# A BF16 ramp of places made once for both layers, and new step orders for layer 1, in a two-layer attention kernel

## The chip, the cores and the metric

The kernel runs on one core of a Trainium2 chip. The core has five engines that run side by side and meet through semaphores: TensorE (PE) for matrix products and transposes, VectorE (DVE) and ScalarE (ACT) for elementwise work, GpSimd (POOL) for elementwise work and indirect transfers, and SyncE (SP), which here only issues transfers. ACT and POOL issue transfers too. The metric is the device time of one execution in microseconds.

## What is computed

Two layers in sequence on x of shape (8, 512, 32, 32), so 8 batches of 512 channels and 1024 tokens. All data is float32. In the reference, cut to what matters:

```python
# layer 0: group norm, 8-head attention over all 1024 tokens, projection, residual
h = group_norm(x, 32 groups) * gn_w + gn_b
q, k, v = split(qkv_w @ h + qkv_b)
x = x + proj_w @ (softmax(q.T k / 8) v) + proj_b

# layer 1: attention among the 256 tokens of greatest norm
q, k, v = wq @ x, wk @ x, wv @ x
importance = sum(x * x over channels)
idx = top_k(importance, 256)
q_sel, k_sel, v_sel = q[idx], k[idx], v[idx]
q_sel, k_sel = layer_norm(q_sel), layer_norm(k_sel)
attended = softmax(clip(q_sel k_sel.T / sqrt(512))) v_sel
v[idx] = attended
out = x + wo @ v
```

## The kernel before, in words

Layer 0 runs as 64 units (4 head pairs x 2 halves of the queries x 8 batches). An order written out by hand, `SLOT`, lists the steps of one unit with an offset of units for each step; each engine gets its instructions in that order. A ring of 14 score buffers (`scored`, tag `e`) holds the exponentials: `sc` takes one, the sum on POOL (L1339) and the product with the values on PE (L1350) give it back. `constants()` is called at the start of unit 2: two small vectors, a triangular mask, and the token numbers (two iotas on POOL, then a copy on DVE, L226). The last units mix in the first steps of layer 1 for batch 0. The last residual additions of layer 0 are at L1121 (tile `xr_last`), its last scaling on POOL at L1402.

Layer 1 runs batch by batch in software pipelining. `BATCH` is the order of one period: a word such as `back4---` is step `back` number 4 of the batch three before, `row4+` that of the batch after. `END` is the order of the last stretch, where batches 4 to 7 are finished (there `row3-` belongs to batch 6, `row1` to batch 7). Both are walked in program order, and every engine takes its own instructions in that order and waits where an input or a buffer is not ready. The steps, with their lines in the profile:

- Rows: `row` transposes 128 tokens (PE, L273), `square` takes their norms (ACT, L277) and `keep` copies them (ACT, L283) into one of four `xT` buffers, `put` stores them to DRAM (issued by ACT, L287, `sx<-xT`). `finite` cleans the norms (DVE), `spread` lays them out as a row (PE, L301), `imp` copies it (ACT, L307).
- Places: `count` (DVE, L320 to L330) counts for each token how many come before it; `place` (DVE, L436) adds the counts; `pick` (DVE, L451) compares a ramp 0..255 with each place, four instructions of 128x256 per step, into BF16 one-hot tiles. The ramp was a float32 tile `iota_f` in a pool of layer 1, written by an iota on POOL (L444) when the first `pick` is reached. `holder` (PE, L459) multiplies the one-hot tiles with the token numbers, `who` (DVE, L467) turns them into indices, `getx` (POOL, L475) gathers the selected rows.
- Values, by seven products of halves: `xs` (POOL, L395) forms sums of token blocks, 8 operations per step, in two alternating halves of a buffer; `va` to `vf` are the products (PE, L405); `ka`, `kb`, `kc`, `ke` copy them (ACT, L419); `kd`, `kf`, `kg` add (DVE, L423); `vput` stores them (issued by ACT, L431), `getv` gathers the selected ones (POOL, L475).
- Attention: `selt`, `selk` (PE L503, ACT L509), `qk` (PE, L519), `stats`, `root`, `norm` (DVE L526 to L529, ACT L534, DVE L541 to L548), `normt`, `scale` (PE L559, ACT L570), `score` (PE, L581), `clip` (DVE, L590 to L594), `exp` (ACT, L602), `probt`, `probk` (PE L614, ACT L619), `att`, `attk` (PE L628, ACT L635), `attput` (SP, L641).
- Output: `fetch` gathers attended rows into the values (POOL, L647), `back` transposes (PE, L663), `add` adds the residual and stores (DVE L671, SP L673).

All PE results of layer 1 go through a ring of eight PSUM banks, handed out in program order: a step that takes a bank waits for the step that emptied it last. `load_x1` (SP, L236) loads the tokens of a batch into buffers that alternate between two sets, at the start of each period.

Of the kernel before, what the change touches and what calls it, by code (L numbers as in the profile page):

```python
# [20 lines left out]
P = 128  # L21
# [44 lines left out]
back6--- row3 square1 xs1 back4--- keep2 square3 back7--- va1 inv-- put2 va0 keep3 put4 row0  # L66
keep1 add6--- ka1 add7--- ka0 put1 put3 att0-- xs0 vb1 vb0 kb0 vc0 row6 square0 kb1 add4---
square6 holder- vd0 who- add3--- kc0 keep6 row7 keep0 row5 square5 kg0 vd1 att1-- keep5 square7
getx- keep7 ve0 finite kf1 kc1 attk1-- kf0 va2 attk0-- xs2 attput-- fetch7-- kd0 fetch4--
spread0 imp0 vc1 fetch3-- ka2 spread1 va3 selt0- imp1 selk0- count1 fetch6-- count7 selt1-  # L70
selk1- fetch2-- vb2 kg1 vf1 fetch5-- vput1- count4 kf2 qk1- ke1 count0 ve1 qk0- qk2- xs3 ka3
put0 stats1- vb3 kd1 root1- back5-- norm1- stats0- kb2 put7 vput2- vput4- fetch1-- count3 vput5-
add5-- stats2- root0- qk3- norm0- vd2 vput7- vput0- stats3- root2- kc2 fetch0-- back1-- kb3
root3- vf0 normt0- vput6- ke0 norm2- vd3 back2-- back0-- normt1- vput3- put5 add1-- scale0-
scale1- vc2 vf2 norm3- normt2- count6 ke2 getv- vc3 normt3- add2-- kc3 kg2 add0-- scale2- kg3
scale3- score0- count2 score1- put6 row4+ square4+ ve3 clip- row1+ row2+ keep4+ ve2 exp0- kd3
vf3 kd2 kf3 probt- count5 place back3-- pick1 square2+ pick0 ke3 probk-
"""
END = """
square1- inv--- row7- keep2- back6---- put4- row6- put2- keep1- square7- xs3- row3- row0-  # L80
att1--- put1- keep7- put7- square3- holder-- add3---- row5- attk1--- va3- keep3- square5- row0
keep5- square0- who-- square6- put5- back7---- back4---- vput2-- add7---- finite- add6----
att0--- keep6- spread0- spread1- getx-- add4---- ka3- imp0- row7 keep0- row1 selt0-- imp1- row4
selk0-- square7 selt1-- kf3- put3- put0- selk1-- keep7 count4- count3- vput7-- square4 square1
put7 keep4 xs2- qk0-- count0- attk0--- stats0-- qk1-- count6- va2- stats1-- keep1 attput---
put6- fetch5--- count5- ka2- root1-- kf2- square0 norm1-- keep0 vput4-- qk2-- vb3- vb2- put1
fetch1--- stats2-- put0 row2 kb2- row6 count2- put4 root2-- square2 vd2- square6 row3 kb3- qk3--
fetch7--- square3 keep2 fetch2--- norm2-- fetch6--- count1- kc2- vf2- root0-- vc2- norm0-- row5
vput6-- ke2- square5 kg2- keep3 normt0-- vd3- keep5 kc3- stats3-- root3-- vput1-- vc3- count7-
va0- ve2- scale0-- fetch0--- vput5-- fetch4--- finite norm3-- normt1-- fetch3--- spread1 kd2-  # L90
ka0- put5 imp1 normt3-- normt2-- xs0- scale3-- spread0 kg3- place- pick1- vf3- scale1-- va1-
keep6 pick0- imp0 back7--- holder- scale2-- score1-- score0-- count5 vb0- back6--- who- ve3-
count3 clip-- kb0- vd0- back0--- ka1- getx- back3--- ke3- vput3-- add6--- kf0- vput0-- xs1- vb1-
add7--- back2--- add3--- kc0- put6 selt0- vf0- vc0- exp0-- add2--- kd3- count6 inv-- selt1-
# [52 lines left out]
def attention_then_topk_attention(  # L147
# [293 lines left out]
    def pick(b, j):  # L441
        if "iota" not in w:
            w["iota"] = pools["up"].tile([P, TOP], F32, tag="iota", name="iota_f")
            nc.gpsimd.iota(  # L444
                w["iota"], pattern=[[1, TOP]], base=0, channel_multiplier=0,
                allow_small_or_imprecise_dtypes=True,
            )
# [1182 lines left out]
```

## Time and profile before

| | |
|---|---|
| median of 4 runs | 2372.77 us (2372.18 to 2372.96) |
| profiled execution | 2370.7 us, span from first to last instruction 2369.0 us |
| busy share of the span | PE 98%, DVE 80%, ACT 62%, POOL 60% |
| mean granted TensorE clock | 0.997 of full |
| layer 1 begins on PE | 1918.28 us from the span's start |
| one steady period of layer 1 | 56.7 us, PE busy 56.54 us of it |

Times in profile lines are microseconds from the span's start, unless a column says ns. In a line of groups or of the timeline stand engine, source line, operation, output and inputs; a square bracket holds the engine's idle time before it and what ended that idle time. In a line of waits stand the waiter, whom it waited for, total us, times, and the longest. The lines themselves are shown in the prediction.

### The profile page before, as it was taken

How to read it: one execution, taken by the hardware profiler on the slowest of the kernel's cores; microseconds unless marked ns; L12 is line 12 of the kernel's file. 1: busy time of each engine (PE TensorE's matmuls, PEld its weight loads, DVE VectorE, ACT ScalarE, POOL GpSimd, SP SyncE). 2: the span in 40 equal slices, each digit the busy share in tenths (PEclk: the TensorE clock that was granted, in tenths of full speed). 3: DMA queues.
4: the chain of work that ended last, by engine and by line, in shares of the span. 5: the costliest groups of instructions: out<-in, count | busy, mean ns of one | idle time of the engine just before them, and what ended most of it. 6: DMA issues, size and time to landing. Idle time of an engine off the chain costs nothing.

```text
span 2369.0 us, 36766 instructions
## 1 busy us (share of the span) xinstructions
PE 2324.0 (98%) x13164; PEld 1053.6 (44%) x13164; DVE 1883.4 (80%) x3019; ACT 1477.9 (62%) x2024; POOL 1432.6 (60%) x890
## 2 busy tenths in 40 slices
PE   7999999999999999999999999999999999999998
PEld 3333443344334333433443344334433357777766
DVE  4889888988888788888988898888777366777774
ACT  3678766776777577657776776677666534444622
POOL 2668655866676677657765776676656634444334
PEclk9999999999999999999999999999999999999999
DMA  5112222322221222222222222221323443666655
GB/s 196 48 44 69 71 77 72 102 63 73 82 91 53 84 79 88 57 79 79 90 68 77 88 79 61 84 68 57 102 79 117 150 158 120 218 223 226 215 170 172
DMA packets 201238, 244.43 MB, mean 103 GB/s; under 512 B 41930, under 2 KB 111306, under 8 KB 201056
## 3 DMA queue, kind: packets, MB, share of 16 engines
q1 hardware_dynamic: 175392, 198.51, 26.4%
q10 hardware_dynamic: 18144, 31.48, 3.6%
q0 software_dynamic: 7520, 12.09, 1.9%
q8 instruction: 105, 1.72, 0.3%
q14 instruction: 77, 0.63, 0.1%
HBM read 181.42 MB, written 73.14 MB: 107 GB/s over the span
## 4 chain that ended last, share of the span: by engine, by line
PE 87%; DVE 6%; ACT 2%; DMA 2%; POOL 1%; issue 1%; another core or an unknown queue 0%; SPq 0%; ACTq 0%; DVEq 0%; POOLq 0%
PE sc L1272 18%; PE av L1350 16%; PE g L1031 14%; PE g L898 10%; PE g L1071 7%; PE b_px L405 5%; PE b_pp L519 4%; DVE high L1286 2%; PE b_py L405 2%; PE den L1366 1%; DVE e L1331 1%; PE b_sc L581 1%; PE b_pa L628 1%; PE first L898 1%; PE b_po L663 1%
## 5 line engine op out<-in xcount | busy, mean ns | idle before, releaser
L1339 POOL TENSOR_TENSOR es<-es,e 128x1024 f32<-128x1024 f32 x384 | 910.9, 2372 | 162.3 <-ACT e L1334 145.4
L1331 DVE TENSOR_TENSOR e<-e,ns 128x1024 f32<-128x1024 f32 x512 | 608.6, 1204 | 6.7 <-ACT ns L1327 6.6
L1280 ACT COPY e<-sc 128x1024 f32<-128x1024 f32 x512 | 501.1, 1016 | 167.1 <-DVE high L1286 98.9
L1334 ACT ACTIVATE e<-e 128x1024 f32<-128x1024 f32 x512 | 533.1, 1062 | 100.2 <-DVE e L1331 93.7
L1286 DVE TENSOR_TENSOR high<-sc,high 128x1024 f32<-128x1024 f32 x384 | 469.0, 1221 | 114.2 <-PE sc L1272 88.9
L1272 PE MATMUL sc<-q,k 64*128 64x512 f32 x2048 | 515.1, 618 | 11.1 <-DVE high L1286 8.6
L1350 PE MATMUL av<-e,v 128*64 128x512 f32 x2048 | 490.2, 597 | 1.1 <-ACT e L1334 0.5
L1339 POOL TENSOR_TENSOR es<-e,e 128x1024 f32<-128x1024 f32 x64 | 152.5, 2383 | 447.4 <-ACT e L1334 447.4
L1272 PEld LDWEIGHTS sc<-q,k 64*128 64x128 f32 x2048 | 173.3, 185 | 285.0 <-issue 151.4
L1350 PEld LDWEIGHTS av<-e,v 128*64 128x64 f32 x2048 | 136.1, 136 | 288.0 <-issue 236.9
L1031 PE MATMUL g<-wqkv,mix_qk 128*64 128x512 f32 x960 | 230.9, 602 | 1.3 <-POOL wqkv L943 1.3
L898 PE MATMUL g<-o,wp 128*64 128x512 f32 x912 | 206.8, 595 | 0.0
L1031 PE MATMUL g<-x,mix_qk 128*64 128x512 f32 x720 | 169.8, 592 | 0.0
L1031 PEld LDWEIGHTS g<-wqkv,mix_qk 128*64 128x64 f32 x960 | 60.9, 136 | 155.3 <-issue 114.2
L898 PEld LDWEIGHTS g<-o,wp 128*64 128x64 f32 x912 | 63.0, 137 | 135.4 <-issue 132.9
L519 PE MATMUL b_pp<-w,selT 128*128 128x512 f32 x256 | 114.2, 593 | 0.0
L1121 DVE SCALAR_TENSOR_TENSOR xr<-g,pb,xr 128x512 f32<-128x512 f32 x56 | 42.1, 751 | 81.5 <-PE g L898 80.7
L1286 DVE TENSOR_TENSOR high<-sc,e 128x1024 f32<-128x1024 f32 x64 | 77.3, 1208 | 34.2 <-ACT e L1280 34.1
L1402 POOL TENSOR_TENSOR o<-o,ri 128x512 f32<-128x512 f32 x64 | 81.7, 1277 | 31.2 <-DMA ri<-rid 29.1
L419 ACT COPY V<-b_px 128x256 f32<-128x256 f32 x112 | 39.8, 374 | 95.7 <-PE b_px L405 89.4
L647 POOL DMA_INDIRECT V<-sa,at x64 | 64.5, 1007 | 56.1 <-DMA sa<-att 27.7
L1031 PEld LDWEIGHTS g<-x,mix_qk 128*64 128x64 f32 x720 | 51.6, 137 | 102.9 <-issue 89.9
(227 smaller groups left out, 2868.9 us busy)
## 6 DMA issues: line engine op xcount, KB each, us to landing
nb<-negd SPq DMA_DIRECT2D x128, 256.0 KB
x<-in_x_dram SPq DMA_DIRECT2D x32, 512.0 KB
ri<-rid SPq DMA_DIRECT2D x128, 128.0 KB
sx<-xT ACTq DMA_DIRECT2D x64, 256.0 KB
mix_qk<-mixd SPq DMA_DIRECT2D x120, 128.0 KB
xr<-in_x_dram SPq DMA_DIRECT2D x58, 256.0 KB
x1d<-xr SPq DMA_DIRECT2D x58, 256.0 KB
sv<-V ACTq DMA_DIRECT2D x56, 256.0 KB
```

Source lines behind the costliest of these rows:

```text
L405: nc.tensor.matmul(out_, left, w["products"][n][:, k], start=(first and k == 0), stop=(k == 1), skip_group_check=True,)
L519: nc.tensor.matmul(pp, tiles["selT", b][:, k, ts(rb, P)], w["qk"[which]][:, k, :], start=(k == 0), stop=(k == CT - 1),)
L898: nc.tensor.matmul(out[r, :], wide_[:, r], moving, start=(k == 0), stop=(k == CT - 1),)
L1031: nc.tensor.matmul(pt[r, :], weights[:, k, r], moving[:, k, :], start=(first and k == 0), stop=(k == 1), skip_group_check=True,)
L1071: nc.tensor.matmul(pt[ts(r, HD), ts(j, P)], tokens[:, k, j * P + r * HD : j * P + r * HD + HD], weights[:, k, :], start=(first and j + k = ...
L1272: nc.tensor.matmul(sc[:, hh, :], ks[p][r, ts(j, P)], qs[p][r, ts(hf, HALF)], start=True, stop=True,)
L1280: nc.scalar.copy(raw[t, j], banks["s", t, j])
L1286: nc.vector.tensor_tensor(high[t], banks["s", t, j], raw[t, 0] if j == 1 else high[t], ALU.max)
L1331: nc.vector.tensor_tensor(raw[t, j], raw[t, j], high[t], ALU.add)
L1334: nc.scalar.activation(raw[t, j], raw[t, j], AF.Exp, scale=QK_SCALE)
L1339: nc.gpsimd.tensor_add(sums[t], raw[t, 0] if j == 1 else sums[t], raw[t, j])
L1350: nc.tensor.matmul(avs[t][HD * hh : HD * hh + HD, :], vs[p // 2][:, j, (p % 2) * P + HD * hh : (p % 2) * P + HD * hh + HD], e[:, hh, :], s ...
```

## The change

The ramp moves into `constants()`: an iota writes it as float32 into a score buffer that is free at that moment, a copy turns it into a BF16 constant tile `places`, and `pick` compares that tile with the places. The iota at the first `pick` and its tile are gone. The scratch tile `four` in layer 0 has one buffer in place of two, which is as large (512 bytes per partition) as `places`. `BATCH` and `END` hold the same steps as before in another order.

```diff
 BATCH = """
-back6--- row3 square1 xs1 back4--- keep2 square3 back7--- va1 inv-- put2 va0 keep3 put4 row0
-keep1 add6--- ka1 add7--- ka0 put1 put3 att0-- xs0 vb1 vb0 kb0 vc0 row6 square0 kb1 add4---
-square6 holder- vd0 who- add3--- kc0 keep6 row7 keep0 row5 square5 kg0 vd1 att1-- keep5 square7
-getx- keep7 ve0 finite kf1 kc1 attk1-- kf0 va2 attk0-- xs2 attput-- fetch7-- kd0 fetch4--
-spread0 imp0 vc1 fetch3-- ka2 spread1 va3 selt0- imp1 selk0- count1 fetch6-- count7 selt1-
-selk1- fetch2-- vb2 kg1 vf1 fetch5-- vput1- count4 kf2 qk1- ke1 count0 ve1 qk0- qk2- xs3 ka3
-put0 stats1- vb3 kd1 root1- back5-- norm1- stats0- kb2 put7 vput2- vput4- fetch1-- count3 vput5-
-add5-- stats2- root0- qk3- norm0- vd2 vput7- vput0- stats3- root2- kc2 fetch0-- back1-- kb3
-root3- vf0 normt0- vput6- ke0 norm2- vd3 back2-- back0-- normt1- vput3- put5 add1-- scale0-
-scale1- vc2 vf2 norm3- normt2- count6 ke2 getv- vc3 normt3- add2-- kc3 kg2 add0-- scale2- kg3
-scale3- score0- count2 score1- put6 row4+ square4+ ve3 clip- row1+ row2+ keep4+ ve2 exp0- kd3
-vf3 kd2 kf3 probt- count5 place back3-- pick1 square2+ pick0 ke3 probk-
+inv-- keep2 vput6- square1 back7--- row3 vput3- back6--- keep1 row6 put2 xs1 square3 va1 put1
+keep3 xs0 att0-- put4 back4--- put3 add3--- ka1 va0 vb1 add4--- ka0 vb0 vc0 kb0 add6--- attk0--
+row5 row7 kb1 holder- kf0 vd0 square6 who- square5 add7--- kf1 kc0 square7 vd1 kg0 row0 square0
+keep0 finite keep6 ve0 getx- att1-- vf0 kc1 spread0 keep5 attk1-- attput-- xs2 vput1- imp0
+spread1 fetch5-- fetch2-- kd0 imp1 vf1 va2 ka2 va3 vc1 count1 ke1 vput0- count0 vb2 kg1 fetch6--
+selt0- selk0- fetch7-- ve1 fetch4-- keep7 fetch0-- selt1- selk1- vput4- count4 vput5- count7
+qk1- kb2 ka3 stats1- qk0- xs3 ke0 put6 back5-- count3 qk2- vput7- qk3- root1- stats0- norm1- vb3
+vc2 put7 root0- stats2- vput2- norm0- kf2 fetch1-- root2- add5-- back1-- stats3- root3- norm2-
+vd2 kc2 add1-- kb3 normt0- normt1- vf2 fetch3-- scale0- put5 back2-- vd3 scale1- norm3- normt2-
+getv- ke2 normt3- back0-- scale2- vc3 kc3 scale3- score1- score0- count2 add0-- put0 add2--
+row4+ kg3 kg2 ve3 square4+ count6 clip- keep4+ row2+ vf3 kd3 ve2 kf3 exp0- row1+ probt- ke3 kd1
+kd2 count5 square2+ place pick1 back3-- probk- pick0
 """
 END = """
-square1- inv--- row7- keep2- back6---- put4- row6- put2- keep1- square7- xs3- row3- row0-
-att1--- put1- keep7- put7- square3- holder-- add3---- row5- attk1--- va3- keep3- square5- row0
-keep5- square0- who-- square6- put5- back7---- back4---- vput2-- add7---- finite- add6----
-att0--- keep6- spread0- spread1- getx-- add4---- ka3- imp0- row7 keep0- row1 selt0-- imp1- row4
-selk0-- square7 selt1-- kf3- put3- put0- selk1-- keep7 count4- count3- vput7-- square4 square1
-put7 keep4 xs2- qk0-- count0- attk0--- stats0-- qk1-- count6- va2- stats1-- keep1 attput---
...
-vb1 add5-- add2-- attput kb1 kf1 vc0 vd0 fetch2 back4- vd1 add7-- kc0 kc1 kf0 vf0 kg0 vc1 add4-
-fetch6 kd3 ve0 back6- fetch3 kg1 ve1 kd0 ke0 back3- back1- add6- fetch4 fetch0 kd1 fetch1 vf1
-vf3 ke1 fetch5 back5- back2- back7- back0- back4 add3- back6 add1- add2- add5- back2 add0- back0
-ke3 fetch7 add7- add4 add6 back5 add2 back1 back7 add0 back3 add5 add7 add3 add1
+keep2- xs3- square1- row3- row7- row6- inv--- put4- att1--- square7- back7---- put2- keep7-
+keep1- row0- put7- holder-- put1- add3---- who-- attk1--- square3- row5- square6- back4----
+getx-- keep3- back6---- att0--- square5- keep5- va3- keep6- add4---- square0- keep0- finite-
+put0- add7---- add6---- put5- row1 put3- spread0- imp0- spread1- row0 imp1- row7 selt0-- square1
+selt1-- selk0-- attk0--- ka3- vput2-- selk1-- attput--- vput4-- count3- va2- keep1 square7 keep7
+xs2- count5- put7 qk0-- square0 count0- fetch6--- qk1-- count6- vput3-- row4 vput7-- stats0--
...
+fetch6- vb1 kb0 add4- vd0 kb1 kf0 vd1 fetch4- kc0 kf1 kc1 add7-- add3-- vf0 vc0 kg0 vc1 ve0 kg1
+kd0 back6- add6- fetch3 fetch6 fetch2 ke0 ve1 fetch4 kd1 back1- add1- vf1 ke1 fetch0 vf3 fetch1
+back2- back5- back7- back0- back3- add5- back4 ke3 add7- add2- add3- back6 fetch5 fetch7 back0
+back2 add0- add4 add6 add0 back7 back3 back5 add7 back1 add5 add1 add3 add2
 """
@@ -209,7 +209,14 @@
     before = const.tile([P, P], F32, tag="before", name="before")
     token = const.tile([P, NB, 2], BF16, tag="token", name="token")
 
-    def constants():
+    places = const.tile([P, TOP], BF16, tag="places", name="places")
+
+    def constants(spare):
+        nc.gpsimd.iota(
+            spare, pattern=[[1, TOP]], base=0, channel_multiplier=0,
+            allow_small_or_imprecise_dtypes=True,
+        )
+        nc.vector.tensor_copy(places, spare)
         w["ln_w"] = vector_of(ln_w, CT, "lw")
         w["ln_b"] = vector_of(ln_b, CT, "lb")
         make_lower_triangular(nc, before, val=1.0, diag=False)
@@ -439,17 +446,11 @@
 
 
     def pick(b, j):
-        if "iota" not in w:
-            w["iota"] = pools["up"].tile([P, TOP], F32, tag="iota", name="iota_f")
-            nc.gpsimd.iota(
-                w["iota"], pattern=[[1, TOP]], base=0, channel_multiplier=0,
-                allow_small_or_imprecise_dtypes=True,
-            )
         for i in range(NB // 2):
             nb = j * (NB // 2) + i
             t = get("rp", ("pick", b, nb), [P, TOP], "pick", NB, BF16)
             nc.vector.tensor_scalar(
-                t, w["iota"], tiles["place", b][:, nb : nb + 1], None, ALU.is_equal
+                t, places, tiles["place", b][:, nb : nb + 1], None, ALU.is_equal
             )
 
     def holder(b, _):
@@ -1305,7 +1306,9 @@
 
 
                 r = high.pop(t)
-                four = sp.tile([BLOCKS, P // BLOCK, BLOCK], F32, tag="four", name=f"four_{t}")
+                four = sp.tile(
+                    [BLOCKS, P // BLOCK, BLOCK], F32, tag="four", name=f"four_{t}", bufs=1
+                )
                 for a in range(P // BLOCK):
                     nc.vector.transpose(four[:, a, :], r[ts(a, BLOCK), :])
                 neg = sp.tile([BLOCKS, BLOCK], F32, tag="neg", name=f"neg_{t}")
@@ -1556,7 +1559,8 @@
                         load_x(1)
                         combine_weights()
                     if t == 2:
-                        constants()
+                        constants(spare("places")[:, :TOP])
+                        scored.give("places")
                     if t == UNITS - 3:
                         load_layer1()
                     for name, ahead, j in order:

```

## The prediction

> **What bounds the kernel now.** Read first: busy time by engine, the chain of waits, then sums over stretches of layer 1 (which begins at 1918 us), then who made TensorE (PE) wait there.
>
> ```profile
> PE 2324.0 (98%) x13164; PEld 1053.6 (44%) x13164; DVE 1883.4 (80%) x3019; ACT 1477.9 (62%) x2024; POOL 1432.6 (60%) x890
> PE 87%; DVE 6%; ACT 2%; DMA 2%; POOL 1%; issue 1%; another core or an unknown queue 0%; SPq 0%; ACTq 0%; DVEq 0%; POOLq 0%
> ```
> PE is busy 98% and carries 87% of the chain. The change leaves PE's work as it is, so only PE's gaps and its clock can move the end.
>
> ```profile
> core 0: us, PE busy (x) PEld busy (x) DVE busy (x) ACT busy (x) POOL busy (x), PEclk, DMA share, GB/s
> 1913.00:1950.00 37.00, 32.49 (x163) 23.48 (x160) 19.67 (x59) 15.56 (x38) 14.64 (x31) 0.91 0.45 156
> 2060.00:2116.70 56.70, 56.54 (x285) 42.33 (x284) 40.04 (x124) 26.64 (x65) 26.32 (x45) 1.00 0.66 223
> 2173.50:2230.00 56.50, 54.43 (x265) 37.22 (x265) 43.27 (x138) 28.91 (x71) 19.30 (x34) 1.00 0.72 247
> 2292.00:2369.00 77.00, 69.69 (x323) 51.09 (x321) 38.33 (x90) 21.29 (x52) 31.14 (x44) 0.97 0.46 151
> ```
> A steady period (row 2) has 0.16 us of PE idle; nothing is to be won there, only lost. The start of layer 1 has 4.5 us of idle and a clock of 0.91; the head of END (row 3) 2.1 us; the last stretch 7.3 us, mostly the drain.
>
> ```profile
> PE b_px L405 <- POOL xs L395: 3.0, 3, 1.2
> PE b_pt L273 <- DVE xr_last L1121: 1.5, 1, 1.5
> 1922.76 0.34 POOL L444 IOTA iota_f<- 128x256 f32 x1 [24.53 <-DMA x<-x1d]
> 1923.07 0.46 POOL L395 TENSOR_TENSOR xs<-x_q,x_k 128x128 f32<-128x128 f32 x1
> 1923.14 3.90 DVE L451 TENSOR_SCALAR pick<-iota_f,place 128x256 bf16<-128x256 f32 x8 [4.25 <-POOL iota_f L444]
> ```
> The start (waits, then timeline; the bracket is the idle time before and what ended it): the iota holds POOL until 1922.76 (four waits of its own, 1919.4 to 1922.6), `xs` is queued behind it, and PE waits three times for `xs`. The picks too wait 4.25 us for it.
>
> ```profile
> 1923.00:1926.00 3.00, 1.82 (x10) 1.06 (x8) 2.86 (x6) 1.16 (x4) 2.84 (x8) 1.00 0.88 332
> 1926.00:1928.00 2.00, 0.76 (x3) 0.36 (x3) 1.05 (x3) 0.00 (x0) 1.92 (x5) 0.93 0.01 4
> 1928.00:1931.00 3.00, 2.45 (x5) 1.55 (x6) 0.00 (x0) 0.04 (x1) 2.40 (x6) 0.50 0.00 0
> 1931.00:1934.00 3.00, 3.00 (x25) 2.45 (x25) 0.00 (x1) 1.66 (x5) 0.00 (x0) 0.50 0.00 0
> 1934.00:1937.00 3.00, 3.00 (x17) 2.68 (x18) 0.75 (x3) 1.92 (x6) 2.04 (x2) 0.91 0.17 25
> ```
> After those gaps (PE busy 2.58 of 5 us) the clock is 0.50, from 1927.7 (0.07 x 2 / 0.5 = 0.28 us before 1928) to 1934.5 (0.09 x 3 / 0.5 = 0.54 us after 1934): 6.8 us.
>
> **The change, part by part.**
>
> *Start of layer 1.* The iota goes from the head of POOL's layer-1 queue. `xs` 1 and 0 are then first there. The loads of their inputs were issued by 1875 (SP's rows); their buffer is the one of layer 0's last values, read until PE's last L1350 at 1895.8; POOL's last layer-0 step (L1402) ends at 1898.2. So 16 operations of 0.46 us (the xs rows) end near 1905.6. PE starts its rows at 1918.28 as before (the 1.5 us wait for xr_last stays); new order: 5 rows x 0.43, va1 and va0 3.46, so vb1 is due at 1923.9: `xs` is 18 us early, and the 3.0 us of waits go. Without the gaps the clock should not fall: of the 6.8 us at half rate 0.55 was idle, and (6.8 - 0.55) / 2 = 3.1 us come back. Check: PE's steps from 1918.28 to the first selt sum to 17.7 us, and selt began at 1942.89, 24.6 us later; 6.9 us were lost there, 6.1 of them are these two terms. What is late next: spread0 of batch 1, at 1931.6 in the new order, needs all eight squares. ACT has 8 row operations until 1923.5 as now, ka/kb to 1926.5, then square6, 5, 7, and 0 after row0 (1929.9), ending 1930.8, `finite` 0.5 more: 1931.3, in time by 0.3 us. The first selt then comes 20.3 us of PE work after 1918.28, at 1938.6; its gather, from holder at 1927.7, has 10.8 us (8.65 now). Term: -6.1, bounds -6.9 and, if `xs` should be queued ahead of the L1402 step and delay the last projection, -4.4.
>
> The Trainium skill, page "TensorE: Matmul & The Clock Gate", Part 1 (the HAM clock gate), has the clock halve after an idle window of about 3.4 us; no gap here is over 1.3 us, and still the row shows 0.50, so the measurement decides. By the page the half rate would have another cause and stay, and the sum below would be -1.0 in place of -4.1.
>
> *Picks.* 64 of them take 341 ns (median; 540 beside `xs`). From a BF16 ramp one costs between the 154 ns of a 128x1 TENSOR_SCALAR (L545) and 341; I take 200, so 1.1 us of DVE time per batch. From placing (2089.36) to holder (2098.80) there are 9.4 us, and DVE idles 4.9 us before `who`: nothing on the path, 0.
>
> The Trainium skill, page "VectorE: DVE Perf Modes", section on the TRN2 errata, has a cycle table that would make it 127 ns (58 + 256/4 cycles at 0.96 GHz, an estimate that no run here shows yet); the sum would be the same.
>
> *Layer 0, slot 2.* The iota (0.34) on POOL and a copy (bounds 0.17, the token CAST, and 0.42, a 128x256 TENSOR_TENSOR) on DVE. The ring of e buffers has one free buffer there, whose last reader is PE's L1350 ending at 123.1; so iota to 123.6, copy to 123.9, then POOL's memset, select and two iotas (0.75) and the token copy to 124.5. DVE now leaves this spot at 122.94: 1.5 us later, with 13 DVE steps queued behind it. ACT's exponentials that need them start at 127.48 now and DVE has two idle spells (0.55, 0.61) before: +0.2, bounds 0 and 1.5. The `four` tile with one buffer is written and read by DVE alone, in order: 0.
>
> *BATCH, steady.* PE work between a step and the step that needs it, summed from 0.43 per row/back/normt, 0.87 per va..vf product, 3.44 per qk: qk3 to normt2 6.5 us before, 6.1 after. In those 6.1 us DVE has to do stats3 1.0, norm2 1.8, add1 0.65, norm3 1.8, and 0.55 left of add5: 5.8. It fits by 0.3 (1.2 before: norm3 ended 2076.68, normt2 began 2077.91). clip waits 1.40 us for PE now; behind norm3 DVE gets count2, two adds, two V sums, count6 (5.9) while PE does 5.6: level. POOL's getx, xs2, fetches keep their order with 12 us before vb2; SP's stores and loads stand between the same steps. Six periods: bounds -0.7 (the 0.16 gaps go) and +1.8 (0.3 each); I take +0.4.
>
> *Head of END.*
>
> ```profile
> PE b_pt L273 <- ACT att L635: 1.4, 1, 1.4
> PE b_po L663 <- ACT xT L283: 0.5, 1, 0.5
> PE b_px L405 <- ACT V L419: 0.7, 1, 0.7
> 2201.71 6.85 DMA sx<-xT
> ```
> Rows of two batches pass through four xT buffers; a square needs a put landed (chain: 6.85 us; another, 2216.25 to 2221.29, 5.0). Before: attk1 stood behind square3, which waited until 2208.64. In the new order attk1 is ahead, so that 1.4 goes. But keep3 now stands behind square3 and square6, and va3 takes keep3's bank: va3 is due 7.3 us after END's start (2201.9), keep3 ends at 8.9: 1.6. spread0 then waits for square0 and `finite`: 1.2. And selk0 stands behind the last batch's square1, which needs put0, issued three steps earlier (12.3): landed 17.3, selk0 done 18.7, qk0 due 16.6: 2.1. Sum 5.0 against 1.4 + 0.5 + 0.7 + 0.6 (small gaps): +1.8. Bounds: puts of 2.26 us (the shortest on the chain, 2228.64) take the last two away, -1.5; 6.85 gives +3.7.
>
> *Tail.* The end hangs on vf3, the last two fetches (4.45 us to land) and backs. One back moves from before vf3 to behind it: -0.4, bounds -1 and +1.
>
> Sum: -6.1 + 0.2 + 0 + 0.4 + 1.8 - 0.4 = -4.1. The profiled execution took 2370.7 us (span 2369.0 and 1.7 around it) and would take 2366.6; the median of the runs is 2.1 above it: 2372.8 - 4.1 = 2368.7.
>
> **Rivals.**
>
> *Puts land quickly in END.* The x_k loads there can start 1.3 us earlier in the new order (vf3 of the batch before frees their tiles earlier), so DMA is freer. The head is then 1.5 us better than now, not 1.8 worse: 2365.4. Against it: DMA is 0.9 busy at 2205 to 2216.
>
> *ACT's queue jams in END (slower).* selk0, selk1, ka3, ka2 all stand behind squares 1, 7, 0 of the last batch, each on a put. If puts take 9 us, qk0 waits 6 us and ka2's bank some 4 more, and the clock falls as at the start, 3.4 us for each of two spells: 3.9 + 4 + 6.8 = 14.7 over the likeliest, 2383.4. It decides from about 7 us of wait with a clock drop. For it: 5.0 and 6.85 are seen. Against: PE has qk0, qk1, va2 (8.6 us) right behind selk0 as cover.
>
> *The start is not won.* If `xs` waits for the same event as the iota, or finite is late, the gaps stay: -4.1 + 6.1 = +2.0, 2374.8. Against: `xs` showed no wait of its own after the iota.
>
> **How the numbers follow.** A measurement of this kernel tells 0.2% (4.7 us, 2368.0 to 2377.5) from no change. Likeliest case 0.50, own range 2366 to 2372 (its bounds partly cancel), 0.2 of it below 2368.0; quick puts 0.22, faster; start not won 0.12, same; jam 0.16, slower. Faster 0.42, same 0.42, slower 0.16. The range 2363.5 to 2379 takes in the first three cases with the outer bounds and part of the jam.
>
> **What would show it.** After: no PE wait for `xs`, clock 1.00 from 1918 to 1950, picks near 0.2 us and starting by 1919; first selt near 20 us after PE's first row; idle per steady period under 0.5; in END's head ACT waits on sx<-xT with PE b_pp waiting for selT. Wrong if PE waits at the start for something else, if the clock is still 0.50 there, or if PE's END idle leaves 1 to 8 us.

## The result and the profile after

The changed kernel has a median of 2375.21 us (40 runs, 2372.65 to 2378.69), the kernel before 2372.9 (60 runs beside it): ratio 1.0009, 95% interval 1.0005 to 1.0014. It is 2.3 us slower, where 4.1 us less was forecast. By the prediction's bound of 0.2% that is no change, though the interval leaves out 1; the time lies inside the range (2363.5 to 2379), but outside the likeliest case's own range (2366 to 2372), and on the other side of zero. The profiled execution took 2375.79 us (span 2374.0), 5.1 more than that of before; single executions of one kernel lie several us apart, so the profile is read by its stages.

In the changed kernel most lines have moved down by 7 in the file ahead of `pick` and by 1 to 3 from there on: row is L280, square L284, keep L290, put L294, spread L308, xs L402, the products L412, ACT's copies L426, DVE's sums L430, pick L452, qk L520, y loads L658, x loads L243.

PE's work is what it was, and less of the chain of waits is PE (83% for 87%). Busy time of the engines, and their shares of the chain:

```profile
PE 2324.1 (98%) x13164; PEld 1053.0 (44%) x13164; DVE 1877.6 (79%) x3020; ACT 1477.0 (62%) x2024; POOL 1432.7 (60%) x890
...
PE 83%; DVE 8%; DMA 3%; issue 3%; ACT 2%; POOL 1%; SPq 0%; DVEq 0%; ACTq 0%; POOLq 0%
```

Sums over stretches of the changed kernel, the columns as in the prediction (the second number is the length, the third PE's busy time):

```profile
1913.00:1950.00 37.00, 32.34 (x175) 23.26 (x172) 18.27 (x65) 16.25 (x40) 11.38 (x20) 1.00 0.55 184
2000.00:2057.00 57.00, 55.45 (x281) 41.65 (x280) 38.17 (x120) 25.30 (x64) 24.52 (x43) 1.00 0.66 219
2057.00:2114.00 57.00, 56.42 (x283) 42.28 (x282) 39.51 (x122) 26.09 (x66) 25.91 (x45) 1.00 0.66 220
2114.00:2171.00 57.00, 55.62 (x278) 41.28 (x276) 38.48 (x120) 25.75 (x64) 25.50 (x44) 1.00 0.66 221
2173.50:2230.00 56.50, 55.08 (x263) 37.12 (x263) 42.91 (x142) 30.47 (x74) 21.59 (x36) 1.00 0.73 245
```

The clock at the start is 1.00, as forecast (0.91 before), yet PE still idles 4.7 us there (4.5 before). The steady stretches, idle for 0.16 us before, now idle 1.55, 0.58 and 1.38.

From the trace's starts of PE's first layer-1 row and of the first `qk` of each batch:

| us | before | after | after less before |
|---|---|---|---|
| first layer-1 row | 1918.28 | 1919.47 | +1.19 |
| first row to first qk | 27.22 | 25.85 | -1.37 |
| first period | 53.26 | 53.25 | 0 |
| next three periods | 56.76, 56.76, 56.76 | 58.57, 57.36, 58.39 | +4.04 |
| qk of the fifth batch to the end | 199.93 | 201.11 | +1.18 |

PE's work from first row to first qk is 20.3 us in the old order (17.7 to the first selt by the prediction's sum, 2.6 behind it) and 22.0 in the new (20.3 and 1.7), so the last stage of the new order has 1.7 us less to do. Lost at the start are therefore 6.9 us before and 3.8 after; the last stage has become 2.9 us worse. The first row comes 1.2 us later behind a spell of half clock in layer 0, which a kernel shows in one execution and not in another (last section).

**The start.** PE's waits in the changed kernel, 1912 to 1950 us:

```profile
PE b_px L412 <- ACT V L426: 2.5, 1, 2.5
PE b_pt L280 <- DVE xr_last L1122: 1.5, 1, 1.5
PE b_pi L308 <- DVE col L302: 0.7, 1, 0.7
```

SP's part of the timeline there in the kernel before (start, length, what is issued):

```profile
1909.79 0.80 SPq L657 DMA_DIRECT2D y<-x1d  x2
1910.70 0.36 SPq L1124 DMA_DIRECT2D x1d<-xr_last  x1
1911.11 0.95 SPq L657 DMA_DIRECT2D y<-x1d  x2
1912.15 0.41 SPq L236 DMA_DIRECT2D x<-x1d  x1
```

And in the changed kernel POOL's, SP's, ACT's and PE's part (in brackets the idle time and what ended it):

```profile
1905.00 0.46 POOL L402 TENSOR_TENSOR xs<-x_k,xs 128x128 f32<-128x128 f32 x1
...
1911.89 7.87 SPq L1125 DMA_DIRECT2D x1d<-xr_last  x3
1921.96 1.74 SPq L658 DMA_DIRECT2D y<-x1d  x4
1923.74 5.69 SPq L243 DMA_DIRECT2D x<-x1d  x4
...
1924.50 2.66 ACTq L294 DMA_DIRECT2D sx<-xT  x2
1927.36 0.65 ACT L426 COPY V<-b_px 128x256 f32<-128x256 f32 x2 [2.27 <-DMA y<-x1d]
...
1927.78 1.99 PE L412 MATMUL b_px<-tvo,xs 128*128 128x256 f32 x8 [2.46 <-ACT V L426]
```

`xs` is done at 1905.5 and PE no longer waits for it. But the y loads, issued from 1909.8 before, now go out at 1921.96, behind the last three stores of layer 0. On ACT two puts take 2.66 us to issue where one takes 0.33 if nothing holds it; the second waits until a y load has landed, `ka1` is the next instruction on ACT, and PE's `vb1` waits for `ka1`.

**The periods.** PE's waits in the second period of the changed kernel:

```profile
PE b_px L412 <- ACT V L426: 1.0, 1, 1.0
PE b_px L412 <- DVE V L430: 0.4, 1, 0.4
PE b_ppt L615 <- ACT s L603: 0.2, 1, 0.2
```

ACT's and PE's part of the timeline in it:

```profile
2032.97 0.58 ACT L290 COPY xT<-b_pt 128x512 f32<-128x512 f32 x1 [0.57 <-DMA x<-x1d]
2035.11 2.19 ACTq L294 DMA_DIRECT2D sx<-xT  x2
2037.64 0.65 ACT L426 COPY V<-b_px 128x256 f32<-128x256 f32 x2 [4.09 <-PE b_px L412]
...
2038.16 1.97 PE L412 MATMUL b_px<-tvo,xs 128*128 128x256 f32 x8 [0.97 <-ACT V L426]
2043.63 1.13 PE L412 MATMUL b_px<-tvo,xs 128*128 128x256 f32 x4 [0.42 <-DVE V L430]
```

Again a put that shares no data with an x load is held until that load has landed (`keep3`, right behind put1, shows it; the put itself issues at 2032.60), put3 is held to 2037.0, and `ka1` (2037.64) and `vb1` follow. (The view puts `ka1`'s idle time down to PE, but in the trace its own waits are passed one by one from 2037.33 on, right behind put3's issue: put3 is what held it.) In the old order `ka1` and `ka0` stood ahead of put1 and put3, so a put that took long hurt nobody. ACT's part in the kernel before (copies, then the two puts):

```profile
2035.33 0.37 ACT L419 COPY V<-b_px 128x256 f32<-128x256 f32 x1 [0.47 <-PE b_px L405]
2037.06 0.37 ACT L419 COPY V<-b_px 128x256 f32<-128x256 f32 x1 [1.35 <-PE b_px L405]
2037.12 1.57 ACTq L287 DMA_DIRECT2D sx<-xT  x2
```

What holds them is a semaphore. The trace records, by number, the semaphores that an instruction waits for, and with a transfer the one that tells of its landing. Of transfers:

| transfer | issued at | waits for the transfers of | its own landing |
|---|---|---|---|
| before, first y load (SP, L657) | 1909.79 | 103, 105, 108 | 105 |
| after, first y load (SP, L658) | 1921.96 | 100, 101, 104, 105, 106, 108 | 100 |
| after, second, third, fourth x load (SP, L243) | 2027.70, 2028.16, 2028.64 | 106, 108, 101 | 106, 108, 101 |
| after, put1, put4, put3 (ACT, L294) | 2032.60, 2035.11, 2036.97 | 106, 108, 101 | 106, 108, 101 |

Transfers of SP and ACT take turns on eight completion semaphores (100 to 106 and 108), and each waits for the one before it on its own: three puts in a row stand behind three x loads, and the wait of put3, issued at 2036.97, is over at 2036.93. And the y tile waits for three more transfers than before; with the iota's tile gone, later tiles of layer 1 lie elsewhere. The theory tested below: the start was won as forecast, then partly lost to the moved tiles, and the new BATCH costs a period 0.6 to 2 us, since puts stand ahead of `ka1` on ACT and `who` and an `add` ahead of `kf1` on DVE. Rivals: the ramp itself costs, END costs, the orders are harmless.

### The profile page after: what moved, and what is told of

Read it like the earlier page. It is cut to its first block, busy times and chain, and to the rows that moved or that the text cites. A ratio compares the mean times of both kernels' runs of the same rounds, so it can differ in the third digit from the quotient of the medians.

```text
span 2374.0 us, 36758 instructions
## 1 busy us (share of the span) xinstructions
PE 2324.1 (98%) x13164; PEld 1053.0 (44%) x13164; DVE 1877.6 (79%) x3020; ACT 1477.0 (62%) x2024; POOL 1432.7 (60%) x890
## 4 chain that ended last, share of the span: by engine, by line
PE 83%; DVE 8%; DMA 3%; issue 3%; ACT 2%; POOL 1%; SPq 0%; DVEq 0%; ACTq 0%; POOLq 0%
PE sc L1273 18%; PE av L1353 16%; PE g L1032 14%; PE g L899 10%; PE g L1072 7%; PE b_px L412 4%; PE b_pp L520 3%; DVE high L1287 3%; DVE e L1334 2%; PE den L1369 1%; PE b_py L412 1%; PE b_sc L582 1%; PE first L899 1%; PE last L899 1%; PE b_pa L629 1%
## 5 line engine op out<-in xcount | busy, mean ns | idle before, releaser
L1342 POOL TENSOR_TENSOR es<-es,e 128x1024 f32<-128x1024 f32 x384 | 910.8, 2372 | 162.6 <-ACT e L1337 146.1
L520 PE MATMUL b_pp<-w,selT 128*128 128x512 f32 x256 | 112.8, 592 | 0.0
L426 ACT COPY V<-b_px 128x256 f32<-128x256 f32 x112 | 39.0, 376 | 86.7 <-PE b_px L412 61.5
L1405 POOL TENSOR_TENSOR o<-o,ri 128x512 f32<-128x512 f32 x64 | 81.7, 1277 | 17.3 <-DMA ri<-rid 16.1
```

Of the source, the lines that this page charges most:

```text
L520: nc.tensor.matmul(pp, tiles["selT", b][:, k, ts(rb, P)], w["qk"[which]][:, k, :], start=(k == 0), stop=(k == CT - 1),)
L1342: nc.gpsimd.tensor_add(sums[t], raw[t, 0] if j == 1 else sums[t], raw[t, j])
```

## The experiments

Each letter is one chip, with its own runs of the kernel before, whose medians were 2371.04 (a), 2373.96 (b), 2369.46 (c), 2370.50 (d) and 2370.56 us (e). One kernel run on two chips gave 0.9965 and 0.9982, another 0.9979 and 0.9981; so differences of 0.1% are read inside one chip or from the stages. "Start" is the time lost between first row and first qk (6.9 before, 3.8 after), "periods" the next three, "last" from the fifth batch's qk to the end. The stages come from one profiled execution of each kernel: those of puts_kf1 and load_late lie at the upper end of their kernel's times, those of ramp_end_new and end_new_again at the lower. hole_end_new and end_new_again are one kernel, and so are ramp_only and ramp_again: their "last" differs by 1.4 and 0.7 us.

| kernel | chip | median, ratio [interval] | start | periods | last |
|---|---|---|---|---|---|
| ramp_only | a | 2366.48, 0.9979 [0.997, 0.9988] | 2.4 | 56.76 x3 | 200.6 |
| orders_only | a | 2377.29, 1.0026 [1.0016, 1.0036] | 6.7 | 58.69, 57.42, 58.55 | 198.8 |
| puts_behind | a | 2373.49, 1.0011 [1.0002, 1.002] | 4.5 | 57.82, 57.46, 57.36 | 198.9 |
| hole_kept | a | 2370.98, 1.0000 [0.9991, 1.0009] | 1.3 | 58.84, 57.38, 58.85 | 199.6 |
| ramp_hole | b | 2367.67, 0.9969 [0.9958, 0.9981] | 0.3 | 56.76 x3 | 203.2 |
| new_mended | b | 2372.05, 0.9990 [0.9981, 0.9999] | 1.2 | 57.88, 57.80, 57.93 | 200.2 |
| hole_end_new | b | 2365.62, 0.9965 [0.9951, 0.9979] | 0.2 | 56.76 x3 | 202.3 |
| y_late | b | 2371.87, 0.9989 [0.998, 0.9998] | 1.6 | 58.71, 57.36, 58.75 | 199.7 |
| kf1_ahead | c | 2368.66, 0.9996 [0.9987, 1.0005] | 1.2 | 58.24, 56.89, 57.98 | 198.9 |
| puts_kf1 | c | 2368.26, 0.9994 [0.9985, 1.0003] | 0.6 | 57.42, 58.65, 58.38 | 200.3 |
| late_old_batch | c | 2367.03, 0.9990 [0.9981, 0.9999] | 1.1 | 56.76 x3 | 201.4 |
| load_late | d | 2369.05, 0.9994 [0.9984, 1.0003] | 1.2 | 57.83, 56.68, 57.90 | 200.1 |
| puts_sp | d | 2366.63, 0.9984 [0.9975, 0.9993] | 0.6 | 56.73 x3 | 199.8 |
| ramp_end_new | d | 2369.34, 0.9998 [0.9989, 1.0007] | 2.4 | 56.76 x3 | 200.6 |
| puts_sp_end_old | e | 2362.72, 0.9969 [0.9957, 0.9981] | 0.6 | 56.73, 56.73, 56.72 | 196.2 |
| puts_sp_old | e | 2362.94, 0.9969 [0.9957, 0.9982] | 0.2 | 56.76 x3 | 199.0 |
| end_new_again | e | 2365.86, 0.9982 [0.9973, 0.9991] | 0.2 | 56.76 x3 | 200.8 |
| ramp_again | e | 2366.01, 0.9981 [0.9971, 0.999] | 2.4 | 56.76 x3 | 199.9 |

### The parts alone

ramp_only: the changed kernel with `BATCH` and `END` of before. orders_only: the kernel before with the new `BATCH` and `END`.

> The BF16 ramp with both of the old orders. Theory (the loss sits in the new BATCH order, where put1, put4 and put3 stand ahead of ka1 in ACT's queue): steady periods stay at 56.8 us, PE's waits for xs at the start of layer 1 (3.0 us) are gone, and the time is 3 to 5 us below the kernel before, 2368 to 2370. A second theory, on memory: with the iota's tile gone from the pool, the residual (y) tiles lie over buffers that layer 0 still stores from, so SP issues the y loads near 1922 us instead of 1910 and put2 and put4 hold ACT's first V copies; then PE waits 1 to 3 us for ACT V at the start and only 1 to 3 us are gained. Rival (the ramp itself costs, in layer 0 or by DVE): same as before or above, 2373 to 2375.

> Both new orders with the F32 iota made in layer 1 as before. Theory (new BATCH order costs): steady periods of 57.4 to 58.6 us instead of 56.8, END about 1 us longer, the waits for xs back: 3 to 6 us above the kernel before, 2376 to 2379. The y loads are issued near 1910 again if the memory theory holds. Rival (orders harmless, the loss is at the start or in layer 0): within 1 us of before, 2372 to 2374.

The change is two changes of opposite sign: the ramp alone gains 5.0 us (0.0021 of 2371; 4.6 by the medians), the orders alone lose 6.2 (0.0026). The ramp costs nothing that shows: its periods are those of before. The orders alone bring the waits for `xs` back (start 6.7) and lengthen the periods as in the changed kernel.

### The moved tiles

hole_kept puts a tile of the old size back; ramp_hole does so with the old orders. y_late leaves the tiles where the change put them.

```diff
     def pick(b, j):
+        if "iota" not in w:
+            w["iota"] = pools["up"].tile([P, TOP], F32, tag="iota", name="iota_f")
+            nc.vector.memset(w["iota"][:, :1], 0.0)
```
```diff
-                for _ in range(4):
-                    residual(*next(loads))
                 for name, b, i in steps:
...
+                    if (name, b, i) == ("put", 1, 3):
+                        for _ in range(4):
+                            residual(*next(loads))
```

> The changed kernel with an unused 128x256 F32 tile (one element per partition is set) left where the iota's tile was, so that the layer-1 pools lie where they did. Memory theory: SP issues the y loads near 1910 us and the x loads of batch 2 from 1912 instead of 1922 and 1924, put3 no longer waits to 1926.8, PE's 2.5 us wait for ACT V at the start goes to under 0.7; steady periods are unchanged; 1.5 to 2.5 us below the changed kernel, 2372.5 to 2374. Rival (the place of the tiles is nothing, only the order of the puts): y loads still near 1922 or, if earlier, the wait stays at 2 us or more, and the time is that of the changed kernel.

> The BF16 ramp with both old orders and the unused tile where the iota's was: neither the moved tiles nor the new orders. Theory: the start loses 6.9 us in the kernel before, 2.4 with the ramp alone, 1.0 to 1.5 here; steady periods 56.76 us; 5 to 6.5 us below the kernel before, and 0 to 1.5 below the ramp alone: ratio 0.9973 to 0.9979. Rival (with the old orders the place of the tiles is nothing): as the ramp alone, 0.9979 to 0.998, with y loads near 1910 us and still 2 us lost at the start.

> The changed kernel, its tiles where the change put them, but the first four y loads are issued behind put3 of batch 1 and not ahead of all of layer 1. Theory (the y tiles lie over buffers that layer 0 stores from, so the y loads are late, and each put takes its turn on a transfer semaphore behind a y load): the x loads of batch 2 go out near 1912 us again, the puts wait for stores landed by 1922, ka1 follows at 1924 to 1925 and PE's wait for ACT V at the start is under 0.8 us, not 2.5; steady periods stay at 57.4 to 58.8: 1.5 to 2.5 us below the changed kernel, ratio 0.9998 to 1.0003. Rival (the puts or ka1 wait for something else that the moved tiles bring): the wait stays near 2.5 us and the time that of the changed kernel, 1.0009.

SP's part of hole_kept's timeline at the start:

```profile
1909.56 0.81 SPq L661 DMA_DIRECT2D y<-x1d  x2
1910.47 0.36 SPq L1128 DMA_DIRECT2D x1d<-xr_last  x1
```

PE's waits there, 1912 to 1950 us:

```profile
PE b_pt L280 <- DVE xr_last L1125: 1.5, 1, 1.5
PE b_px L412 <- ACT V L426: 0.7, 1, 0.7
```

An unused tile of 1 KB per partition brings the y loads back to 1909.6 and takes PE's wait from 2.5 to 0.7 us; the start loses 1.3 instead of 3.8. With the old orders the loss falls from 2.4 to 0.3: 6.6 us better than before, where 6.1 were forecast for the whole start. y_late mends the start (1.6) with the tiles moved, by issuing the y loads behind the puts. So the moved tiles act through the late y loads; its ratio is lower than expected (0.9989 for 0.9998 to 1.0003), though its stages are as expected.

### The new BATCH

puts_behind moves three puts; new_mended adds the kept tile and kf0, kf1 behind vd0, vd1; kf1_ahead is hole_kept with kf1 moved; puts_kf1 is both moves of the diff with the tile kept. The diff shows only the words that move; the rest of `BATCH` is left out.

```diff
-keep1 row6 put2 xs1 square3 va1 put1 keep3 xs0 att0-- put4 back4--- put3 add3--- ka1 va0 vb1
-add4--- ka0 vb0
+keep1 row6 put2 xs1 square3 va1 keep3 xs0 att0-- back4--- add3--- ka1 va0 vb1
+add4--- ka0 put1 put4 put3 vb0
...
-kf0 vd0 square6 who- square5 add7--- kf1
+kf0 kf1 vd0 square6 who- square5 add7---
```

> The changed kernel with put1, put4 and put3 moved from ahead of ka1 to right behind ka0 in BATCH. Theory (puts that wait for another transfer hold ACT, ka1 stands behind them, PE waits for ACT V): PE's waits for ACT V of 1.0 and 0.8 us in every other steady period are gone (those periods fall to 57.3 to 57.6 us), that of 2.5 us at the start falls below 1; 3 to 5 us below the changed kernel, 2370 to 2372. Rival (ka1 waits for the memory of its V tile, not for the puts): the start keeps its 2.5 us, about 2 us gained. Rival (DVE's order or clock is the cause): the same as the changed kernel, 2374.5 to 2376.

> The changed kernel with three amends: the unused tile kept, put1, put4, put3 behind ka0, and kf0 and kf1 behind vd0 and vd1 in BATCH. Theory: each step between a producer and vb1 or vd0 was a price of the new order (a wait of 1.0 us on ACT's copy in two periods, 0.42 us on DVE's sum in all, each with about 0.25 us for the refilling of PE's pipeline), so steady periods return to 56.8 to 57.0 us, the start loses about 1.3 us instead of 3.8, END stays about 1 us longer: 4 to 5 us below the kernel before, ratio 0.998 to 0.9985. Rival (the new order costs in ways that these waits don't show, or moving the puts delays the squares): periods of 57.3 or more, 1 to 2 us below the kernel before.

> The changed kernel with the unused tile kept and one more edit: kf1 stands right behind kf0 in BATCH, ahead of who and add7 of the older batches. Theory (PE's 0.42 us wait before vd1 is for kf1, which stands on DVE behind the sum of add7, 0.69 us, itself after who's wait of 1.29 us for PE): the wait is gone, the period that has only this wait falls from 57.4 to 56.8 us, the two that also wait for ACT's copies from 58.8 to 58.1; over six periods some 4 us, so 3 to 4.5 us below the kernel before, ratio 0.998 to 0.9988. Rival (the wait is for vd0's bank or kf0): periods unchanged, ratio 1.0.

> As the last, and put1, put4, put3 behind ka0: all three amends of the changed kernel that the waits point to (tile, puts, kf1). Theory: every steady period 56.8 to 57.1 us, start loss about 1.3 us against 6.9, so 5.5 to 7 us below the kernel before, ratio 0.997 to 0.9978, level with the best of the old BATCH. Rival (later puts hold back squares and finite, and DVE's kd and kg with them): periods of 57.3 or more, ratio above 0.9985.

The kf1 wait is settled. DVE in hole_kept, where kf1 is the fourth line:

```profile
2095.94 0.16 DVE L471 TENSOR_REDUCE who<-b_pn 128x2 f32<-128x4 f32 x1 [1.29 <-PE b_pn L463]
2096.14 0.17 DVE L473 CAST who<-who 128x2 uint32<-128x2 f32 x1
2096.22 0.69 DVE L675 TENSOR_TENSOR y<-b_po,y 128x512 f32<-128x512 f32 x1
2096.83 0.41 DVE L430 TENSOR_TENSOR V<-b_px,V 128x256 f32<-128x256 f32 x1
```

With kf1 ahead of these the period that had only this wait falls from 57.38 to 56.89. A listed wait of 0.42 us cost 0.49: it is the gap between two records, and in a stream the records overlap (in the changed kernel groups of four begin at 2035.30 and 2036.16, 0.86 us apart, and each is listed with 1.03); a wait undoes this overlap too. The three periods came out as expected, 2.0 us less in sum; the expectation of the time counted six of them, and there are three.

Moving the puts took PE's waits for ACT's copies out of the periods of puts_behind, as expected (58.57 and 58.39 became 57.82 and 57.36), but its time did not fall: the start lost 0.7 more, PE there waiting 2.2 us for a DVE sum. In puts_kf1 the rival came true, by its stages and by its ratio of 0.9994. ACT, DVE and PE in its third period:

```profile
2097.50 0.60 ACT L284 ACTIVATE xT<-b_pt 128x512 f32<-128x512 f32 x1 [2.24 <-DMA sx<-xT]
...
2098.09 0.36 ACT L426 COPY V<-b_px 128x256 f32<-128x256 f32 x1
...
2098.48 0.42 DVE L430 TENSOR_TENSOR V<-b_py,V 128x256 f32<-128x256 f32 x1 [2.48 <-ACT V L426]
...
2098.96 1.13 PE L412 MATMUL b_py<-w,xs 128*128 128x256 f32 x4 [1.70 <-DVE V L430]
```

A put issued later lands later, the square that takes its xT buffer holds ACT 2.24 us, the copy `kc0` is behind that square, `kg0` on DVE behind the copy, `ve0` on PE behind `kg0`. new_mended failed in the same place, with kf1 late as well.

load_late and puts_sp start from kf1_ahead. The first issues the x load behind put3 of each period and no longer at its head, the second gives the puts of batches 1 to 7 to SP:

```diff
-                if 1 <= t:
-                    steps.append(("load", t + 1, 0))
...
+                    if 1 <= t and (name, ahead, i) == ("put", 0, 3):
+                        steps.append(("load", t + 1, 0))
```
```diff
-        nc.scalar.dma_start(x_dram[b][ts(j, P), :], tiles["xT", b, j])
+        (nc.sync if b else nc.scalar).dma_start(x_dram[b][ts(j, P), :], tiles["xT", b, j])
```

> The changed kernel with the tile kept and kf1 ahead of who, and the load of the next x issued behind put3 instead of at the head of each period. Theory (put4 and put3 take their turn on the transfer semaphores right behind the x load of an even batch, 512 KB a piece, 8 us to land, and so hold ACT's copy ka1): PE's waits for ACT V in two of the three profiled periods (2.4 us in sum) go, periods 56.8 to 57.2 us, 5.5 to 7 us below the kernel before, ratio 0.997 to 0.9978. Rival (the puts wait for DMA bandwidth or for their rows, not for the load): the two periods stay near 58 us and the ratio near 0.9996.

> The changed kernel with the tile kept and kf1 ahead of who, and the puts of layer 1 issued from SP's queue instead of ACT's. Theory (ACT is held by its own waiting puts, ka1 stands behind them): no wait of PE for ACT's copies in the periods, 56.8 to 57.2 us each, since a put that waits now holds SP, whose loads and stores have time; 4 to 7 us below the kernel before unless END's puts come late on SP; ratio 0.997 to 0.9985. Rival (the copies are late for another reason): periods near 58 us as before this edit.

> Both old orders with the ramp, the tile kept and the puts on SP. In the old order ka1 and ka0 stand ahead of put1 and put3 and PE has work until vb1, so the theory gives the puts' move nothing in the periods (56.76 us) and at most 0.5 us at the start or in END: ratio as the ramp and the tile alone, 0.997 to 0.998. Rival (puts on SP are better by themselves, so that the gain in the mended new order says nothing on ka1): periods below 56.7 or END over 2 us shorter.

load_late told nothing: SP has little ahead of the load, issued it at 2024.92, still before the puts, and the periods stayed within 0.4 us. Its rival's sign, two periods near 58 us, came, but the edit did not part the load from the puts. puts_sp is clear. PE's waits over all its periods, in the window 1950 to 2172 us:

```profile
PE b_ppt L618 <- ACT s L606: 0.7, 4, 0.2
```

With the puts off ACT the new order runs at 56.73 us a period, 0.03 below the old one. So the puts on ACT, and kf1, are the whole loss of the new BATCH. puts_sp_old has 56.76 as before: in the periods the puts hurt only an order in which `ka1` stands behind them. Whether puts on SP also help in END is open: its last stage is 0.9 us shorter than that of the kernel before, and 4.2 shorter than that of ramp_hole, its pair but for the puts (over the 2 us that its expectation named), but the two ratios are equal, and in ramp_hole's profile ACT stood idle 4.8 us at 2225 us for a cause that the profile calls remote, and PE 2.7 us behind it. What holds a put is the semaphore that it shares with the load (the table of semaphores above); the load's bandwidth enters only through the time that the load takes to land. The Trainium skill, page "DMA: Bandwidth & Descriptors", section "Anatomy of one DMA — SWDGE (gpsimd) path", says that any semaphore wait of a transfer happens on the sequencer that issues it, before dispatch. The trace agrees for ACT: two issues took 2.66 us there, and its copy stood behind them.

### The new END

hole_end_new (and end_new_again, the same kernel) is ramp_hole with the new END, ramp_end_new is ramp_only with it, late_old_batch y_late with the old BATCH, puts_sp_end_old puts_sp with the old END.

> The ramp, the unused tile and the new END with the old BATCH. Theory: the new END costs 0.5 to 1.5 us against the old one (the comparison of the profiles gives 1.0, the prediction had 1.4), so 4 to 5.5 us below the kernel before and about 1 us above the kernel with old END, ramp and tile: ratio 0.9977 to 0.9983. Rival (END is where the loss came from): no better than the kernel before.

> The old BATCH, the new END and the ramp, no unused tile, the first four y loads behind put3 of batch 1. Theory (what the moved tiles cost is only the lateness of the y loads, so issuing them late where nothing stands behind them mends it as well as the tile did): start loss 1 to 2 us, periods 56.76 us, ratio 0.9965 to 0.9975. Rival (the moved tiles cost in other places): ratio 0.998 or more, as the ramp alone with both old orders (0.9979).

> The ramp, the old BATCH, the new END, and the tiles where the change put them: the change without its new BATCH. Theory: start loss about 2.4 us as with the ramp alone, periods 56.76 us, END as in the other kernels with the new order: 4 to 6 us below the kernel before, ratio 0.9975 to 0.9985. Rival (only with the kept tile is there a gain with the new END): ratio 0.999 or more.

> The mended new BATCH (tile kept, kf1 ahead of who, puts on SP) with the old END. Against the same kernel with the new END this shows END alone. Theory (the new END is level with the old one to about 1 us): 2366 to 2368, 2.5 to 5 us below the kernel before, ratio 0.998 to 0.999. Rival (the new END costs 2 us or more, which would explain why the ramp with it alone came out at 0.9998): ratio 0.997 to 0.9978.

> The kernel with the best ratio so far (ramp, tile kept, old BATCH, new END; 0.9965) beside the others on one chip. If the theory's stage sums hold (start 6.5 us better, periods the same, END 0.5 to 1.5 worse), 5 to 6 us below the kernel before: 0.9975 to 0.998. Rival: the earlier ratio leaned on slow runs of the kernel before, and it is 0.9985 or more.

> The ramp alone with both old orders, the tiles moved, beside the others on one chip. Theory (start loss 2.4 us against 6.9, nothing else): 4 to 5 us below the kernel before, 0.9979 to 0.9984, and 1 to 2 us above the kernels with the tile kept. Rival (the ratio differs more between chips than its interval says): outside 0.997 to 0.999.

On chip b the new END is level with the old one (2365.62, lower than expected, and 2367.67, intervals overlapping). On the mended new BATCH the last stage is 3.6 us shorter with the old END, and the median 3.9 us lower (puts_sp and puts_sp_end_old, on two chips whose kernels before are level); the rival of that expectation, 2 us or more, came true. PE's waits from 2172 to 2292 us in puts_sp, the longest:

```profile
PE b_pi L308 <- DVE col L302: 0.6, 1, 0.6
PE b_po L667 <- DVE s L596: 0.6, 1, 0.6
PE b_px L412 <- ACT xT L290: 0.6, 1, 0.6
PE b_st L507 <- DMA sel<-sx,who: 0.6, 1, 0.6
```

And in puts_sp_end_old:

```profile
PE b_pt L280 <- ACT att L639: 0.9, 1, 0.9
PE b_po L667 <- ACT xT L290: 0.5, 1, 0.5
PE b_st L507 <- DMA sel<-sx,who: 0.4, 1, 0.4
```

So the new END trades the wait for `attk1` for a wait on `finite` and longer ones on keep and the gather. Waits are not all: for the same products from the fifth batch's qk on, PE is busy 187.9 us in puts_sp and 186.2 in puts_sp_end_old, 189.3 in end_new_again and 188.0 in puts_sp_old (these two differ in the puts as well). So in these pairs the new END costs 1.3 to 1.7 us of PE's own time, for a reason that was not looked for, and 0.5 to 1.9 us of idle. The other pairs, as they stand, give -0.9 (chip b) and 0 to 0.7 (ramp_end_new against ramp_only and ramp_again), but there the profiles with the old END are disturbed: ramp_hole by the idle time of ACT named above, ramp_only and ramp_again by 3.4 us of half clock at 2207 us, which costs up to 1.7.

ramp_end_new at 0.9998 is not explained by its stages, which are those of ramp_only; they come from an execution 1.9 us under its median. late_old_batch, too, is above its expectation, with its first row at 1920.84 us behind a spell of half clock in layer 0. puts_sp_end_old (2362.72) and puts_sp_old (2362.94) are the best of all: 7.8 and 7.6 us below the kernel before on chip e.

## Why the prediction was wrong, point by point

- **Start, -6.1.** The mechanism was right: no wait for `xs`, which ended at 1905.5 for 1905.6 forecast; clock 1.00; 6.6 us back with the tiles unmoved and the old orders, 5.6 with the new. `xs` even ran ahead of layer 0's last scaling (L1405 at 1903.77) without harm. The changed kernel got 3.1. The step that failed is "ka/kb to 1926.5": it took ACT's copies to follow the rows and did not count put1, put4 and put3 ahead of `ka1`, nor that removing a tile moves others; `ka1` came at 1927.36, and PE waited 2.5 us. The small term for `finite`, "in time by 0.3 us", missed by 1.0: PE waited 0.7 us. By the prediction's own sign, "Wrong if PE waits at the start for something else", the start went wrong. That the clock stayed at 1.00 behind a wait of 2.5 us was luck (last section).
- **BATCH, steady, +0.4, bounds -0.7 and +1.8.** The main error: +4.0 in three periods. "SP's stores and loads stand between the same steps" looked at SP; the puts are issued by ACT. The sum followed qk3 to normt2, where nothing went wrong, and not `ka1` to `vb1` and `kf1` to `vd1`, where less PE work now lies between. It also counted six periods; the trace has three steady ones, and a first of 53.3 us that stayed as it was.
- **Head of END, +1.8, and tail, -0.4.** attk1's wait went, as forecast. Of the three new waits (which add up to 4.9, where the prediction has 5.0) two came, smaller: PE waited 0.7 us for keep (1.6 forecast) and 0.5 ahead of spread0 (1.2); `qk0` did not wait for `selk0` (2.1). In the 60 us behind the fifth batch's qk PE idles 1.4 us, 2.1 before: the head is no worse. The stage is 2.9 us worse all the same: 1.55 us more idle in the 120 us behind the head (the gather 1.1 of it), 0.85 more in the tail, and 1.1 us more of PE's own time, half clock included. The forecast of 1.4 for both terms is off, but inside their bounds. ACT's queue did jam, but in BATCH, behind puts, and not in END behind squares.
- **Picks, 0.** One takes 275 ns (median), where 200 was taken. Nothing on the path waits for it. The estimate of 127 ns by the cycle table of the Trainium skill, page "VectorE: DVE Perf Modes", section on the TRN2 errata, is not met; the measurement decides.
- **Layer 0, +0.2.** Not visible beside a spell of half clock. With the ramp the first row lies between 1917.17 and 1918.80 in the nine profiles without a spell of half clock at 1856 to 1864 us, and between 1918.28 and 1920.84 in the nine with it; without the ramp, and without the spell, it lies at 1918.28 and 1918.74.
- **The total.** Start and periods together miss by 6.6 us and the time by 6.4 (2.3 against -4.1). That these agree so well is partly chance: in the two profiles, which lie 5.1 us apart, the last stage adds 1.5 over its forecast and layer 0 another 1.0. The time also lies beside that of the rival "The start is not won" (2374.8), by luck: half of what was forecast for the start was won, and the loss came from the periods and END.

## What to carry to other kernels

A transfer issued from an engine that also computes is an instruction in that engine's order: in a new order, look at what stands behind each of them and which unrelated transfer it takes its turn behind. When a tile is removed, see what now lies over memory that is still being read, and keep its place free while you measure the rest. Run the two halves of a mixed change apart: here -5.0 and +6.2 us hid behind +2.

## What the runs showed of the hardware

The clock can halve without a long gap, and not each time. In layer 0, PE idles 1.8 us before the den products, and of 18 profiles of kernels with the ramp 9 then show a low clock between 1856 and 1864 us; ramp_only has none, ramp_again, the same kernel, has it. (The two profiles without the ramp have none, too few to tell.) PE's part of the timeline there in the changed kernel:

```profile
1856.50 0.64 PE L1369 MATMUL den<-es,ones 128*32 128x256 f32 x8 [1.82 <-POOL es L1342]
1857.32 5.40 PE L345 MATMUL g<-w,x 128*128 128x512 f32 x8 [0.18 <-ACT xT L290]
```

And in ramp_only:

```profile
1856.51 0.64 PE L1369 MATMUL den<-es,ones 128*32 128x256 f32 x8 [1.83 <-POOL es L1342]
1857.07 3.70 PE L345 MATMUL g<-w,x 128*128 128x512 f32 x8
```

The eight products take 1.7 us more. On the other hand the one gap of 2.46 us at the start of layer 1 was followed by full clock, where three gaps of at most 1.2 us in the kernel before were followed by half. The length of the last gap does not decide it.

The traces show what does. In each of the 20 profiles the records of the granted clock begin whole multiples of 3.413 us apart: the 6.8 us at 0.50 in the kernel before are two such steps. What counts is how much of one step PE is busy:

| profile | step, us | PE busy of 3.41 us | clock in the next step |
|---|---|---|---|
| before | 1924.33 to 1927.74 | 1.19 | 0.50 |
| after | 1923.10 to 1926.52 | 2.23 | 1.00 |
| after | 1926.52 to 1929.93 | 2.15 | 1.00 |
| after | 1854.84 to 1858.25 | 1.57 | 0.50 |
| ramp_only | 1855.20 to 1858.61 | 2.10 | 1.00 |
| ramp_again | 1852.53 to 1855.95 | 1.59 | 0.50 |

The gap of 2.46 us in the changed kernel happened to straddle the end of a step (1926.52), so that each of the two steps kept over 60% of PE work; the short gaps of the kernel before fell into one step. From 60 us on, the 20 profiles hold 13 466 steps at full clock. All 35 in which PE was busy less than 42% were followed by half clock, none of those above 47% was, and of 11 in between 4 were. Back to full clock it went behind each step at 0.50 in which PE was busy over 82%, and behind none under 81%. Where the steps lie differs from one execution to the next, so one kernel can lose a step of clock in one run and not in another.
